# Three edits to a sparse graph transformer: attention credit at the layer border, one block weighted on VectorE, and the order of the last matmuls

## The chip, the cores and the metric

The kernel runs on one core of one Trainium2 chip. A core has five engines, each with its own instruction queue: TensorE (PE, with a separate row PEld for weight loads), VectorE (DVE), ScalarE (ACT), GpSimd (POOL) and SyncE (SP), which only issues DMAs here. Engines wait for each other through semaphores. The metric is device time in microseconds (us) of one execution.

## The reference

Two layers of the same form over 2708 tokens of 512 values, in f32, with 8 heads of 64 and a feed-forward width of 2048. A token attends to its neighbours in a graph and to itself; under 24 positions a row are open in the sparse matrix that the inputs give.

```python
def _L0_gnn_ref(h, adj, ...):
    n = h.shape[0]
    mask = adj.astype(jnp.float32) + jnp.eye(n, dtype=jnp.float32)
    q = (h @ Wq.T + bq).reshape(n, N_HEADS, D_K)
    k = (h @ Wk.T + bk).reshape(n, N_HEADS, D_K)
    v = (h @ Wv.T + bv).reshape(n, N_HEADS, D_K)
    scores = jnp.einsum('nhd,mhd->hnm', q, k) / jnp.sqrt(jnp.float32(D_K))
    scores = jnp.where(mask[None, :, :] == 0, jnp.float32(-1000000000.0), scores)
    attn = jax.nn.softmax(scores, axis=-1)
    ctx = jnp.einsum('hnm,mhd->nhd', attn, v).reshape(n, D_MODEL)
    h1 = _layer_norm(h + ctx @ Wo.T + bo, ln1_g, ln1_b)
    ff = jax.nn.relu(h1 @ W1.T + b1) @ W2.T + b2
    return _layer_norm(h1 + ff, ln2_g, ln2_b)
...
x = _L0_gnn_ref(x, adj, ...)
x = _L1_gnn_ref(x, adj, ...)
```

## The kernel before

**Tiles and slots.** A first part turns the adjacency into neighbour lists of at most 24 slots, sorts the tokens by their number of neighbours, and cuts them into 22 tiles of 128 (the last, tile 21, holds 20). Each tile has a number of slots that all its tokens fit into: tile 21 has 3, 20 has 5, 19 has 6, 18 has 7, 9 has 9, 8 has 10. Tiles go in pairs, called blocks; `blocks` is (21,20), (19,18), (8,9), (7,10), (6,11), (0,17) and so on, 11 in all. A second way over all pairs of tokens stands behind a flag and isn't executed.

**Attention** is not a matmul here. For each tile, chunk by chunk of two slots (`SLOTS`), POOL gathers the key and value rows of those neighbours into a buffer `kv` (L982, five buffers, up to three gathers ahead). DVE multiplies the keys by the query (L1019) and sums over each head (L1025), which gives scores `sc`. ACT takes exponentials (L1038) into `p`. The values are then weighted by `p`: slot 0 by one DVE product of 128x512 (L1051), slot 1 by eight ACT copies with a scale, one for each head (L1045). DVE adds the result to `acc` (L1058). At the end of a tile come the sum over slots (L1066), the largest score (L1070), the sum of `p` (L1078) and its reciprocal (L1081), and ACT divides (L1089) into `cx`. The generator `attend` issues these in a pipeline: in each step the scores of one chunk, the weighting of the chunk before, the sums of the one before that, the division of the one before that.

**Dense work** is on PE. `query` projects q into a PSUM buffer of the tag "g" (three buffers), evicts it by DVE (L1226) into a "row" buffer `qs` (three buffers, shared with `xb`), and `kept` stores it to DRAM by SP (L1236, `q_d`) when the next query is issued. `attended` turns `cx` (`flip`, tp L1128, ACT L1133) into cT, projects it with Wo (L569), and adds the residual xb (loaded at L979, added at L1254), and `norm` follows: statistics L1112 to L1116, a power on POOL L1118, and the two passes L1119 and L1122. `feed_forward` makes 16 steps f: matmuls pf (L1296), relu ft on ACT (L1304), and, three steps later (`LAG`), `second` (L1284) into one PSUM accumulator for each tile of the block. The last three steps follow tile by tile. Then come add (L1316), norm, and in the last layer the store of the output (L1319).

**How the two are woven together.** Code order is queue order on PE, ACT and SP everywhere; on POOL in the first part and layer 0; on DVE only in the first queries and at the border between the layers. Elsewhere a scheduler orders DVE. Between dense pieces the kernel calls `advance(x)`: x is added to a credit (at most 1.5), and `attend` makes steps until it is used up; a chunk of two slots costs 1, one of a single slot 0.5. No step is made while two finished `cx` wait to be used. At the border, the head of layer 1, there is one `advance(0.5)` before each of the queries (L1491 and L1494), whose zT come from DRAM by SP (L1213):

```python
while pool:
    advance(0.5)
    now.query(*pool.pop(0))
for i in range(2 * AHEAD - 10):
    advance(0.5)
    next(streamed)
through(0)
early[n] = now.attended(blocks[0], got)
```

`through(0)` makes attention steps until both tiles of the first block are divided.

Of the kernel before, what the change touches and what calls it, by code (L numbers as in the profile page):

```python
# [19 lines left out]
DM = 512  # L20
NH = 8
DK = DM // NH
# [3 lines left out]
NFC = FF // P  # L26
# [12 lines left out]
LAG = 3  # L39
# [432 lines left out]
def by_edges(ctx: ExitStack, tc: tile.TileContext, x, xT, adj, layers, out, good):  # L472
# [13 lines left out]
    NL = len(layers)  # L486
# [94 lines left out]
    def size(g):  # L581
        return min(P, N - g * P)
# [425 lines left out]
    class Tile:  # L1008


        def __init__(self, g, q):
            self.g, self.r, self.q = g, size(g), q
            self.sc = at.tile([P, LIST, NH], F32, tag="sc", name="sc", bufs=2)
            self.p = at.tile([P, LIST, NH], F32, tag="p", name="p", bufs=2)
            self.acc = None
# [16 lines left out]
        def weigh(self, kv, s0, c):  # L1032
            r, g, p = self.r, self.g, self.p
            if s0 == 0:
                self.acc = at.tile([P, SLOTS, DM], F32, tag="acc", name="acc", bufs=2)
                self.wide = c
            for s in range(s0, s0 + c):
                nc.scalar.activation(  # L1038
                    p[:r, s, :], self.sc[:r, s, :], AF.Exp, bias=minus[:r, g, s : s + 1]
                )  # L1040
            to = self.acc[:r] if s0 == 0 else kv[:r, :, DM:]
            for i in range(1, c):
                for h in range(NH):
                    hd = slice(h * DK, (h + 1) * DK)
                    nc.scalar.activation(  # L1045
                        to[:, i, hd],
                        kv[:r, i, DM + h * DK : DM + (h + 1) * DK],
                        AF.Copy,
                        scale=p[:r, s0 + i, h : h + 1],
                    )  # L1050
            nc.vector.tensor_tensor(  # L1051
                to[:, 0, :].rearrange("p (h d) -> p h d", d=DK),
                kv[:r, 0, DM:].rearrange("p (h d) -> p h d", d=DK),
                p[:r, s0, :].unsqueeze(2).to_broadcast([r, NH, DK]),
                ALU.mult,
            )
            if s0:
                nc.vector.tensor_tensor(  # L1058
                    self.acc[:r, :c, :], self.acc[:r, :c, :], kv[:r, :c, DM:], ALU.add
                )  # L1060
# [76 lines left out]
    class Layer:  # L1137
# [133 lines left out]
        def feed_forward(self, block, hs, hT):  # L1271

            w = sum(size(g) for g in block)
            accs = [ps_a.tile([P, DM], F32, tag=f"a{i}", name=f"a{i}") for i in range(len(block))]
            fts = []

            def second(f, only=None):
                c0 = 0
                for g, a in zip(block, accs):
                    r = size(g)  # L1280
                    if only not in (None, g):
                        c0 += r
                        continue
                    nc.tensor.matmul(  # L1284
                        a[:r],
                        fts[f][:, c0 : c0 + r],
                        self.w2[f // 2][:, f % 2, :],
                        start=(f == 0),
                        stop=(f == NFC - 1),
                    )  # L1290
                    c0 += r

            for f in range(NFC):
                pf = ps_f.tile([P, DM], F32, tag="f", name="pf")
                for c in range(NC):
                    nc.tensor.matmul(  # L1296
                        pf[:, :w],
                        self.w1[f // 2][:, c, f % 2 * P : f % 2 * P + P],
                        hT[:, c, :w],
                        start=(c == 0),  # L1300
                        stop=(c == NC - 1),
                    )
                ft = dn.tile([P, 2 * P], F32, tag="ft", name="ft", bufs=4)
                nc.scalar.activation(ft[:, :w], pf[:, :w], AF.Relu, bias=self.b1[:, f : f + 1])  # L1304
                fts.append(ft)
                if f >= LAG:
                    second(f - LAG)
                yield None
            for g in block:
                for f in range(NFC - LAG, NFC):  # L1310
                    second(f, g)
            zs = []
            for g, a, h in zip(block, accs, hs):
                r = size(g)
                z = h
                nc.vector.tensor_tensor(z[:r], a[:r], h[:r], ALU.add)  # L1316
                norm(z, r, self.g2, self.e2)
                if self.n == NL - 1:
                    nc.gpsimd.indirect_dma_start(  # L1319
                        out=out,  # L1320
                        out_offset=bass.IndirectOffsetOnAxis(ap=ident_i[:r, g : g + 1], axis=0),
                        in_=z[:r],
                        in_offset=None,
                        bounds_check=N - 1,
                        oob_is_err=False,
                    )
                zs.append(z)
            yield zs
# [41 lines left out]
    blocks = [(NT - 1, NT - 2), (NT - 3, NT - 4)] + [  # L1370
        (i, NT - 5 - i) for i in (*range(8, 5, -1), *range(6))
    ]
# [3 lines left out]
    def attend(n, got):  # L1376

        peak = small.tile([P, NT], F32, tag="peak", name="peak", bufs=1)
        nc.vector.memset(peak, 0.0)
        loaded = loads(n)  # L1380
        steps = []
        for g in order:
            cuts = chunks_of(g)
            steps += [(g, s0, c, i, i + 1 == len(cuts)) for i, (_, s0, c) in enumerate(cuts)]
            if g == order[1]:
                steps += [None] * 3
        steps += [None] * 3
        kv = next(loaded)
        yield 0.0
        q = asked(n, order[0])  # L1390
        done = [None] * 3
        for k, step in enumerate(steps):
            if step:
                g, s0, c, i, last = step
                if i == 0:
                    while q is None:
                        q = asked(n, g)
                        if q is None:
                            yield None
                    t, q = Tile(g, q), None  # L1400
                if k > 0:
                    kv = next(loaded)
                t.weights(kv, s0, c)
                if i > 0 and q is None and g != order[-1]:
                    q = asked(n, order[order.index(g) + 1])
                done.append((t, kv, s0, c, last))
            else:
                done.append(None)
            t3, t2, t1 = done[-4:-1]
            if t1:  # L1410
                t1[0].weigh(*t1[1:4])
            if t2 and t2[-1]:
                t2[0].sums(peak)
            if t3 and t3[-1]:
                got[t3[0].g] = t3[0].divided()
            yield c / SLOTS if step else 0.2
        nc.vector.tensor_reduce(flags[:, 4 + n : 5 + n], peak, AX.X, ALU.max)
        nc.vector.tensor_scalar(
            flags[:, 4 + n : 5 + n], flags[:, 4 + n : 5 + n], SAFE, None, ALU.is_le
        )  # L1420
# [3 lines left out]
    def advance(more):  # L1424

        nonlocal credit
        credit = min(credit + more, 1.5)
        while credit > 0 and len(got) < CXB - 1:
            cost = next(ahead, None)
            if cost is None:  # L1430
                break
            credit -= cost

    def through(k):

        while blocks[k][-1] not in got:
            next(ahead)
# [40 lines left out]
    for n in range(NL):  # L1478
        last = n == NL - 1
        nxt = None if last else Layer(n + 1, layers[n + 1])  # L1480
        if n > 0:
            streamed = now.queries(order[8 : 2 * AHEAD])
            got = {}
            ahead = attend(n, got)
            with tc.manual_schedule(engines={mybir.EngineType.DVE}):
                for _ in range(2):
                    now.query(*pool.pop(0))
                next(ahead)
                next(streamed)
                while pool:  # L1490
                    advance(0.5)  # L1491
                    now.query(*pool.pop(0))
                for i in range(2 * AHEAD - 10):
                    advance(0.5)  # L1494
                    next(streamed)
                through(0)
                early[n] = now.attended(blocks[0], got)
                next(early[n])
                for _ in blocks[0]:
                    next(early[n])  # L1500
                finish(streamed)
            now.load_w2(NFC // 2 - 1)
# [6 lines left out]
        for k, block in enumerate(blocks):  # L1509
# [4 lines left out]
            for f, zs in enumerate(now.feed_forward(block, hs, hT)):  # L1514
# [22 lines left out]
                if not last:  # L1537
# [7 lines left out]
                    if f == 1 and k in (1, 3):  # L1545
                        i, name, scale = (1, "bk", 1.0) if k == 1 else (0, "bq", DK**-0.5)
# [97 lines left out]
```

## Time and profile before

| | us |
|---|---|
| median of 3 runs | 1966.08 (1964.01 to 1967.41) |
| the profiled execution | 1964.63 |
| its span in the profile | 1962.9 |
| PE busy | 1901.0 |
| DVE busy | 1300.8 |
| ACT busy | 933.8 |
| POOL busy | 796.8 |

What one operation costs, from the page's groups (line, engine, operation, tiles, form, count, then busy us, mean ns of one, and idle time of the engine before them with what ended most of it):

```profile
L982 POOL DMA_INDIRECT kv<-kv_d,idx x420 | 546.1, 1300 | 475.9 <-DVE acc L1058 319.1
L1045 ACT ACTIVATE kv<-kv,p 128x64 f32<-128x64 f32 x1232 | 311.0, 335 | 5.0
L1058 DVE TENSOR_TENSOR acc<-acc,kv 128x1024 f32<-128x1024 f32 (+2 forms) x178 | 204.0, 1146 | 26.7 <-ACT kv L1045 25.9
L1051 DVE TENSOR_TENSOR kv<-kv,p 128x512 f32<-128x512 f32 (+1 forms) x178 | 121.6, 684 | 52.8 <-ACT p L1038 52.7
```

PE, DVE and PEclk by 40 slices of the span (49 us each; tenths, 9 is 90% or more):

```profile
PE   8999988999999999999999998999999999999997
DVE  5884587685867869659442036888688988877421
PEclk9999999999999999999999999999999999999998
```

The slices with an 8 or a 7 on PE are the first, the sixth and seventh (245 to 343 us, layer 0's first block), the 25th (1178 to 1227, the border of the layers), and the last. An instruction that is reported busy may run at a lower clock: PEclk tells of the mean over a slice, and short drops show only in windows of 10 us. The first block of layer 0 ends at about 346 us.

### The profile page before, as it was taken

What the parts mean: (1) busy time and instruction counts of PE and PEld (TensorE: products, weight loads), DVE (VectorE), ACT (ScalarE), POOL (GpSimd) and SP (SyncE); (2) the same over time, 40 slices, a digit from 0 to 9 for tenths busy, and PEclk for the clock granted to TensorE, in tenths of its full rate; (3) what the DMA queues carried; (4) which work ended last, traced back from release to release, by engine and by line L of the source; (5) the groups of instructions that cost most, each with busy time, mean ns of one, the idle gap of its engine ahead of it and who ended that gap; (6) DMA issues with size and microseconds to landing.
All of it is one profiled execution on the core that took longest, in us unless ns stands there. A gap on an engine that the chain in (4) does not pass through costs nothing. (4 is left out here: it accounts for less than half of the span.)

```text
span 1962.9 us, 20872 instructions
## 1 busy us (share of the span) xinstructions
PE 1901.0 (97%) x6162; PEld 1100.6 (56%) x6162; DVE 1300.8 (66%) x2142; ACT 933.8 (48%) x3219; POOL 796.8 (41%) x710
## 2 busy tenths in 40 slices
PE   8999988999999999999999998999999999999997
PEld 4444444565565655566556643556666566666664
DVE  5884587685867869659442036888688988877421
ACT  4660254564555655547332112756456765755410
POOL 3114635453555535425310022555347655644210
PEclk9999999999999999999999999999999999999998
DMA  9998766455655556546310646856455766554000
GB/s 327 352 311 307 258 211 235 161 166 189 202 161 199 188 186 227 161 150 204 130 43 27 230 162 215 298 174 217 153 177 198 247 214 209 186 190 154 34 11 13
DMA packets 131486, 366.92 MB, mean 187 GB/s; under 512 B 16668, under 2 KB 36988, under 8 KB 128654
## 3 DMA queue, kind: packets, MB, share of 16 engines
q0 software_dynamic: 69120, 246.35, 37.9%
q1 hardware_dynamic: 53332, 99.66, 14.9%
q10 hardware_dynamic: 8910, 19.48, 2.6%
q8 instruction: 50, 0.82, 0.2%
q14 instruction: 74, 0.61, 0.1%
HBM read 314.62 MB, written 50.83 MB: 186 GB/s over the span
## 5 line engine op out<-in xcount | busy, mean ns | idle before, releaser
L982 POOL DMA_INDIRECT kv<-kv_d,idx x420 | 546.1, 1300 | 475.9 <-DVE acc L1058 319.1
L1284 PE MATMUL a<-w,ft 128*128 128x512 f32 (+1 forms) x1408 | 669.9, 601 | 10.8 <-ACT ft L1304 9.5
L1296 PE MATMUL pf<-hT,w 128*128 128x256 f32 (+1 forms) x2816 | 636.3, 373 | 13.2 <-ACT ft L1304 8.8
L1296 PEld LDWEIGHTS pf<-hT,w 128*128 128x128 f32 x2816 | 521.1, 191 | 192.2 <-issue 107.3
L1284 PEld LDWEIGHTS a<-w,ft 128*128 128x128 f32 (+1 forms) x1408 | 256.5, 187 | 239.0 <-issue 201.4
L1304 ACT ACTIVATE ft<-pf,b 128x256 f32<-128x256 f32 (+1 forms) x352 | 158.5, 459 | 424.8 <-PE pf L1296 424.5
L1019 DVE TENSOR_TENSOR kv<-kv,q 128x1024 f32<-128x1024 f32 (+3 forms) x222 | 256.5, 1158 | 156.3 <-DMA kv<-kv_d,idx 103.7
L1045 ACT ACTIVATE kv<-kv,p 128x64 f32<-128x64 f32 x1232 | 311.0, 335 | 5.0
L1025 DVE TENSOR_REDUCE sc<-kv 128x16 f32<-128x1024 f32 (+3 forms) x222 | 255.2, 1154 | 1.4
L1058 DVE TENSOR_TENSOR acc<-acc,kv 128x1024 f32<-128x1024 f32 (+2 forms) x178 | 204.0, 1146 | 26.7 <-ACT kv L1045 25.9
L1118 POOL TENSOR_TENSOR rd<-va,mhalf 128x1 f32<-128x1 f32 (+1 forms) x88 | 85.4, 971 | 267.6 <-DVE va L1116 266.2
L1038 ACT ACTIVATE p<-sc,minus 128x8 f32<-128x8 f32 (+1 forms) x420 | 103.4, 295 | 161.1 <-DVE sc L1025 154.6
L569 PE MATMUL o<-wo,cT 128*128 128x512 f32 (+1 forms) x352 | 157.8, 601 | 3.7 <-DVE qs L1226 3.3
L1051 DVE TENSOR_TENSOR kv<-kv,p 128x512 f32<-128x512 f32 (+1 forms) x178 | 121.6, 684 | 52.8 <-ACT p L1038 52.7
L569 PEld LDWEIGHTS o<-wo,cT 128*128 128x128 f32 (+1 forms) x352 | 65.5, 187 | 92.2 <-issue 80.9
L1089 ACT ACTIVATE cx<-acc,su 128x64 f32<-128x64 f32 (+1 forms) x352 | 88.4, 333 | 42.6 <-DVE su L1081 33.9
L1316 DVE TENSOR_TENSOR h<-a,h 128x512 f32<-128x512 f32 (+1 forms) x44 | 29.7, 677 | 106.8 <-PE a L1284 106.7
L1122 DVE SCALAR_TENSOR_TENSOR h<-h,rd,ln_b 128x512 f32<-128x512 f32 (+1 forms) x88 | 65.9, 749 | 50.9 <-POOL rd L1118 50.9
L663 ACT ACTIVATE code<-aj 128x2708 bf16<-128x2708 int32 (+1 forms) x22 | 73.2, 3329 | 49.1 <-POOL aj L659 45.4
L1355 POOL DMA_INDIRECT kv_d<-kvs,ident_i x22 | 23.7, 1077 | 179.0 <-ACT kvs L1349 110.9
L666 DVE MAX8 tops<-code 128x8 f32<-128x247 f32 (+2 forms) x242 | 83.1, 400 | 19.3 <-ACT code L663 19.3
L1045 ACT ACTIVATE acc<-kv,p 128x64 f32<-128x64 f32 (+1 forms) x352 | 88.8, 334 | 1.4
(133 smaller groups left out, 1514.2 us busy)
## 6 DMA issues: line engine op xcount, KB each, us to landing
aj<-in_adj SPq DMA_DIRECT2D x21, 1354.0 KB, 8.0
kv_d<-kvs ACTq DMA_DIRECT2D x21, 512.0 KB, 5.6
w<-in_W SPq DMA_DIRECT2D x20, 512.0 KB, 4.8
xg<-in_xT SPq DMA_DIRECT2D x19, 512.0 KB, 8.8
kv<-kv_d,idx POOLq DMA_INDIRECT x420, 5.6
w<-in_W ACTq DMA_DIRECT2D x12, 512.0 KB, 8.9
q_d<-qs SPq DMA_DIRECT2D x22, 256.0 KB, 4.2
zT_d<-zT SPq DMA_DIRECT2D x22, 256.0 KB, 5.3
```

Of the source, the lines that this page charges most:

```text
L569: nc.tensor.matmul(o[:r], xs(c), wm[:, c, :], start=(c == 0), stop=(c == NC - 1))
L982: nc.gpsimd.indirect_dma_start(out=to, out_offset=None, in_=table[:, :], in_offset=bass.IndirectOffsetOnAxis(ap=s, axis=0), bounds_check=N ...
L1019: nc.vector.tensor_tensor(kv[:r, :c, :DM], kv[:r, :c, :DM], self.q[:r].unsqueeze(1).to_broadcast([r, c, DM]), ALU.mult,)
L1025: nc.vector.tensor_reduce(self.sc[:r, s0 : s0 + c, :], kv[:r, :c, :DM].rearrange("p s (h d) -> p s h d", d=DK), AX.X, ALU.add,)
L1038: nc.scalar.activation(p[:r, s, :], self.sc[:r, s, :], AF.Exp, bias=minus[:r, g, s : s + 1])
L1045: nc.scalar.activation(to[:, i, hd], kv[:r, i, DM + h * DK : DM + (h + 1) * DK], AF.Copy, scale=p[:r, s0 + i, h : h + 1],)
L1051: nc.vector.tensor_tensor(to[:, 0, :].rearrange("p (h d) -> p h d", d=DK), kv[:r, 0, DM:].rearrange("p (h d) -> p h d", d=DK), p[:r, s0, : ...
L1058: nc.vector.tensor_tensor(self.acc[:r, :c, :], self.acc[:r, :c, :], kv[:r, :c, DM:], ALU.add)
L1089: nc.scalar.activation(cx[:r, hd], self.acc[:r, 0, hd], AF.Copy, scale=self.su[:r, h : h + 1])
L1284: nc.tensor.matmul(a[:r], fts[f][:, c0 : c0 + r], self.w2[f // 2][:, f % 2, :], start=(f == 0), stop=(f == NFC - 1),)
L1296: nc.tensor.matmul(pf[:, :w], self.w1[f // 2][:, c, f % 2 * P : f % 2 * P + P], hT[:, c, :w], start=(c == 0), stop=(c == NC - 1),)
L1304: nc.scalar.activation(ft[:, :w], pf[:, :w], AF.Relu, bias=self.b1[:, f : f + 1])
```

## The change

It has three parts. At the border both `advance(0.5)` become `advance(0.4)`. A tile gets a flag `alone`, true for the tiles of the second block (19 and 18) in layer 0: DVE then weighs all the slots of a chunk in one product (128x1024 instead of 128x512), and ACT makes no copies for it. And in the last block of the last layer, in the last step f = 15, `second(12)` is issued for the first tile alone; the second tile's f = 12 is issued ahead of its 13, 14 and 15, after all of the first tile's.

```diff
@@ class Tile
-        def __init__(self, g, q):
+        def __init__(self, g, q, alone=False):
             self.g, self.r, self.q = g, size(g), q
+            self.alone = alone
@@ Tile.weigh
             to = self.acc[:r] if s0 == 0 else kv[:r, :, DM:]
-            for i in range(1, c):
+            e = c if self.alone else 1
+            for i in range(e, c):
                 for h in range(NH):
...
             nc.vector.tensor_tensor(
-                to[:, 0, :].rearrange("p (h d) -> p h d", d=DK),
-                kv[:r, 0, DM:].rearrange("p (h d) -> p h d", d=DK),
-                p[:r, s0, :].unsqueeze(2).to_broadcast([r, NH, DK]),
+                to[:, :e, :].rearrange("p s (h d) -> p s h d", d=DK),
+                kv[:r, :e, DM:].rearrange("p s (h d) -> p s h d", d=DK),
+                p[:r, s0 : s0 + e, :].unsqueeze(3).to_broadcast([r, e, NH, DK]),
                 ALU.mult,
             )
@@ feed_forward
                 if f >= LAG:
-                    second(f - LAG)
+                    very_last = self.n == NL - 1 and block == blocks[-1] and f == NFC - 1
+                    second(f - LAG, block[0] if very_last else None)
                 yield None
             for g in block:
-                for f in range(NFC - LAG, NFC):
+                for f in range(NFC - LAG - (very_last and g != block[0]), NFC):
                     second(f, g)
@@ attend
-                    t, q = Tile(g, q), None
+                    t, q = Tile(g, q, n == 0 and g in blocks[1]), None
@@ the border
                 while pool:
-                    advance(0.5)
+                    advance(0.4)
                     now.query(*pool.pop(0))
                 for i in range(2 * AHEAD - 10):
-                    advance(0.5)
+                    advance(0.4)
                     next(streamed)
```

## Prediction

> **What bounds the kernel now.** I read the page first: span, busy shares, PE's slices.
>
> ```profile
> span 1962.9 us, 20872 instructions
> PE 1901.0 (97%) x6162; PEld 1100.6 (56%) x6162; DVE 1300.8 (66%) x2142; ACT 933.8 (48%) x3219; POOL 796.8 (41%) x710
> ```
>
> PE is busy in 97% of the span, so 1962.9 − 1901.0 = 61.9 us is all that can be won without taking matmuls away, and the change takes none away. Then the waits of PE, to see who ends that idle time:
>
> ```profile
> PE a L1284 <- ACT ft L1304: 9.5, 9, 2.8
> PE pf L1296 <- ACT ft L1304: 8.8, 4, 3.5
> PE tp L1128 <- DVE h L1122: 4.3, 2, 3.9
> PE o L569 <- DVE qs L1226: 3.3, 1, 3.3
> PE q L569 <- DVE qs L1226: 2.9, 2, 1.7
> ```
>
> (us in total, times, longest.) They sit where the three edits sit. So I read PE's timeline in those places; brackets hold the idle time before an entry and its releaser. Layer 0, first block's feed-forward:
>
> ```profile
> 277.66 2.34 PE L1296 MATMUL pf<-hT,w 128*128 128x148 f32 x8 [2.81 <-ACT ft L1304]
> 279.93 3.90 PE L1284 MATMUL a<-w,ft 128*20 128x512 f32 x4
> 293.35 1.79 PE L1296 MATMUL pf<-hT,w 128*128 128x148 f32 x8 [3.45 <-ACT ft L1304]
> 299.62 1.27 PE L1296 MATMUL pf<-hT,w 128*128 128x148 f32 x8 [1.38 <-ACT ft L1304]
> 333.12 1.11 PE L1128 MATMUL tp<-ident,h 128*128 128x128 f32 x4 [3.86 <-DVE h L1122]
> 334.17 7.58 PE L1284 MATMUL a<-w,ft 128*20 128x512 f32 x12
> ```
>
> A long stall costs twice: eight pf matmuls take 1.17 us elsewhere in this block, but 2.34 and 1.79 behind the stalls of 2.81 and 3.45. The layer border, all engines:
>
> ```profile
> 1201.47 1.22 DVE L1226 SCALAR_TENSOR_TENSOR qs<-q,bq 128x512 f32<-128x512 f32 x2
> 1202.13 0.32 SPq L1236 DMA_DIRECT2D q_d<-qs  x1
> 1202.15 3.70 PE L569 MATMUL q<-wq,zT 128*128 128x512 f32 x8 [1.21 <-DVE qs L1226]
> 1209.23 0.69 DVE L1226 SCALAR_TENSOR_TENSOR qs<-q,bq 128x512 f32<-128x512 f32 x1 [5.83 <-DMA q_d<-qs]
> 1210.07 6.30 PE L569 MATMUL o<-wo,cT 128*20 128x512 f32 x8 [3.27 <-DVE qs L1226]
> 1210.39 1.66 SPq L979 DMA_DIRECT2D xb<-xb_d  x2
> 1216.41 0.68 DVE L1254 TENSOR_TENSOR h<-o,xb 20x512 f32<-20x512 f32 x1 [6.49 <-PE o L569]
> 1227.33 1.01 PE L1128 MATMUL tp<-ident,h 20*128 20x20 f32 x8
> 1228.88 4.31 PE L1296 MATMUL pf<-hT,w 128*128 128x148 f32 x32 [0.54 <-ACT hT L1133]
> ```
>
> Read this as one chain: a query evicted at 1201.47 is stored at 1202.13; its buffer ("row", three of them) is free at 1209.23, when the last query can be evicted; only then has o (1210.07) a PSUM buffer. The tail:
>
> ```profile
> 1942.51 7.03 PE L1284 MATMUL a<-w,ft 128*128 128x512 f32 x16
> 1947.01 0.69 DVE L1316 TENSOR_TENSOR h<-a,h 128x512 f32<-128x512 f32 x1 [47.81 <-PE a L1284]
> 1950.62 0.68 DVE L1316 TENSOR_TENSOR h<-a,h 128x512 f32<-128x512 f32 x1
> ```
>
> [...] stalls of 2.81, 3.27, 3.45 and 3.86 are followed by slow matmuls (o: 6.30 for 3.70), those of 1.21, 1.38 and 1.74 hardly. [...] That is how attention reaches PE here: relu (ft) stands in ACT's queue behind exponentials that wait for DVE's scores. [...] The trace has means of 684 (L1051) and 1146 to 1158 (L1058, L1019, which mix in a few narrower ones); I use the trace.
>
> **Part two, block (19,18) by DVE alone.** Tile 19 has three chunks of two slots, tile 18 three of two and one of one: six products grow from 128x512 to 128x1024. Their pitch on DVE is 0.60 now (295.08 to 295.68), that of a 128x1024 operation 1.14 (292.21, 293.34, 294.48): 6 × 0.54 = +3.2 us on DVE. Off ACT go 6 × 8 = 48 copies, 2.02 us a set, pitch about 1.93: −11.6 us. No cover is assured: DVE is 10.0 of 10 busy in 270–280. The instruction orders show the same sets on PE, POOL and SP, and on DVE a few exchanges in this stretch: the second weighting of tile 18 goes before the score reduction of the next tile, 8. Replayed step by step:
> - The first product lies before L1122 at 263.57: feed-forward starts 0.54 later (265.49 to 266.0).
> - Two more make tile 18's first scores 0.5 to 1 late; but the eight copies ahead of the relu at 277 are gone: stall of 2.81 to about 2.1. The division of tile 19 is 0.75 late, so the next relu is 0.8 late: a new stall of about 2.6.
> - Tile 8's gather is issued 0.6 late and lands at 288.65 for 288.10; its score now also waits for one weighting (1.13): its exponentials at 292.15 for 290.49. The relu behind them: PE goes on at 295.0 for 293.35. The following stall (299.62) moves by about +1.1 to +1.7. Up to here PE loses some 1.5.
> - In exchange that weighting ends earlier, so its accumulation ends at 293.25 for 294.56 and frees a kv buffer 1.3 sooner. Through POOL's gathers tile 9's first chunk lands at 315.7 for 316.92, and DVE reaches L1122 (332.31) 1.2 earlier.
> - PE at 333.12 waits for just that, and its 3.86 us of idle swallow the 1.5 lost before: tp at 331.9.
>
> Net −1.2. What follows (the slow a x12, 7.58 for about 5.3) could give 2.4 more if the stall of now some 1.5 spares the clock; I count none of it, since PE waits for a kvs eviction of the same DVE chain at 376. Bounds: −3 (clock spared and kept), +2.5 (buffer comes no earlier, the extra DVE time enters most of the way).
>
> **Part one, 0.4 at the border.** DVE is ordered by hand there, so smaller credit moves instructions: one eviction qs goes ahead of nine DVE instructions of a chunk and a finished tile. PE's, POOL's, SP's and ACT's orders stay, so no DMA issue is moved past another.
> - That qs runs right behind the qs of 1195.34 and the accumulation's end, at 1197.1 for 1201.47, as q is ready. Two 0.67 us evictions no longer follow each other at 1201.47; the q of 1202.15 starts when the 16 before it end (1193.84 + 7.10): 1200.95. −1.2.
> - Its store is issued at 1197.8 for 1202.13. Now it took 1209.23 − 1202.13 = 7.1 to free the buffer; the same from 1197.8 is 1204.9, when the last query (1200.95 + 3.70 = 1204.65) is just ready. So the last qs runs at 1204.9, not 1209.23.
> - The attention instructions go behind it; the division (1201.63) is 0.65 later, its ACT work at 1204.9 for 1206.24 anyway. o starts at 1205.7 for 1210.07, with an idle time too short to slow the clock: 3.44 for 6.30; end 1209.15 for 1216.37.
> - What is late next: h needs xb too. The two xb loads need "row" buffers of qs whose stores go out at 1202.9 and 1203.9, 6 to 7 us each: loads at 1209 to 1210 (now 1210.39), landing by an estimate of 4 us from the median of such loads and stores (4.2 to 5.3 on the page) at 1213 to 1214. So h at 1213.6, not 1209.3: −2.8. The last o and the 16 q matmuls (1216.83, 1220.37) don't wait for h: q ends near 1220.3, tp follows at 1221.7 behind both norms and the next qs, pf at 1222.75 for 1228.88.
>
> −6.1. Bounds: −3 if the stores land late, so that h binds at 1216; −7 if xb is early and the 16 q bind alone.
>
> **Part three, the tail.** One f32 second matmul of 512 is two records of 0.43, so 0.86. Tile 0's sum ends 0.86 earlier (its add at 1946.15 for 1947.01), tile 1's where it was (1942.51 + 7.03 = 1949.54). Tile 1's add stood at 1950.62 behind tile 0's L1122 of 1949.95, not behind PE; so it comes at 1949.76, still after 1949.54. −0.86; bounds −0.5 and −0.9.
>
> **Sum.** −1.2 − 6.1 − 0.9 = −8.2. The profiled execution took 1964.63 (span 1962.9 and 1.7 around it): 1956.4. The median shown is 1.45 above it: 1957.9, rounded 1958.
>
> **Rivals.**
> - A, the border's gain is capped: the stall moves from the qs store to the stores ahead of xb, which land late while DMA is 0.88 busy (1200–1210). For: 7.1 us for a store is far above the median 4.2. Against: in 1210–1220 DMA share is 0.22. Border −2, others −1: 1963. 17%.
> - B, the work of PE before the border is early, but attention's gathers set layer 1's pace, so the gain comes back as waits of 1 to 3 us (there are some at 1430, 1520, 1620), or block 0 loses what the border gains: 1964 to 1968, centre 1966. For: those waits exist. Against: PE is hardly idle for 200 us behind the border, long enough for attention to lead. 13%.
> - C, slower: DVE carries block 0's chain. The +3.2 enters whole, [...] With three more slow stretches at 2.9: 3.2 + 8.7 = +11.9, less 7.0 of the others: +4.9, 1971. It decides once block 0 loses over 7.0 and is slower beyond measuring at 10.9. For: DVE at 10.0 of 10, the new 2.6 stall. Against: 3.86 us of PE idle at 333 that absorb it, and 11.6 us off ACT. 10%.
> - D, block 0 spares its clock and keeps it, border at its best: −3 − 7 − 0.9 = −10.9: 1955. 12%.
>
> **Numbers.** The forecast 48%, A 17, B 13, C 10, D 12. About 0.2% (3.9 us) is what a measurement of this kernel can tell from no change: faster means under 1962.2, slower over 1970. Faster: 48 + 12 + about 8 of A + 2 of B = 70%; slower: 9 of C + 1 of B = 10%; same 20%. Range 1954 to 1965: it holds the forecast's own bounds, D's and A's, and leaves out C and most of B.
>
> **What would show it.** Right: the last qs of the border near 1205, o at full clock behind under 1.5 us idle, pf some 6 us earlier relative to the span; a last L1316 0.9 earlier; in block 0 a tp wait for h under 2 us. Wrong: slow matmuls (PEclk under 0.9) in more slices of 270–300 than now; h at the border waiting for xb to 1216; later waits on ft or q_d in layer 1 that give the 6 us back.

## The result, and the profile after

| | before | after |
|---|---|---|
| median of 13 runs each | 1966.74 us | 1962.70 us |
| lowest and highest | 1963.51, 1970.56 | 1956.50, 1966.42 |
| the profiled execution | 1964.63 | 1965.94 |

The ratio is 0.9974, with a 95% interval of 0.9964 to 0.9985: the change saves 5.1 us by the ratio (3.0 to 7.1), 4.0 by the medians. The forecast was 1958, thus 8.2 us less; direction and range held, and the gain by the ratio is about six tenths of that, by the medians half. In a later set of runs, on another occasion, the same kernel had a ratio of 0.9988 (0.9977 to 0.9998).

The profiled execution of the changed kernel is one of its slowest, 1.3 us longer than that of before. So spans can't be compared; stretches can. PE's matmuls stand in the same order in both kernels up to the last 16, so matmul number k of one trace can be laid beside number k of the other. How much later each begins than in the profile before (us):

```
matmul   at (before)   what begins there                  after is later by
    0         4.9      first key projection                     -0.2
  488       212.2      first part, near its end                 +1.4
  627       264.1      just ahead of block 0's feed-forward     +1.7
  728       299.6      block 0, behind its ft stalls            +4.6
  852       339.9      block 0, behind its tp stall             +2.4
 3595      1185.6      queries of the border                    +6.5
 3680      1228.9      layer 1, first pf                        +0.7
 6145      1942.9      second of the last 16 matmuls            +2.4
```

Read it downwards: what matters is the change from line to line. Of the 6.5 us that after is late at 1185, 1.7 come from the first part, which the change doesn't touch, 0.8 from block 0, and about 4 from the feed-forward blocks behind it. Between 1185 and 1230 it wins 5.8. First the page and PE's waits of after:

```profile
span 1964.1 us, 20821 instructions
PE 1901.4 (97%) x6162; PEld 1101.5 (56%) x6162; DVE 1304.3 (66%) x2142; ACT 922.6 (47%) x3171; POOL 796.8 (41%) x710
```

```profile
PE pf L1298 <- ACT ft L1306: 10.6, 3, 7.5
PE a L1286 <- ACT ft L1306: 10.0, 9, 2.8
PE tp L1130 <- DVE h L1124: 4.4, 3, 2.5
PE q L569 <- DVE qs L1228: 2.3, 1, 2.3
```

(Line numbers are one to three higher than before.) DVE is busy 3.5 us more, ACT 11.2 less: 3.2 and 11.6 were forecast. The wait of o for qs, 3.3 us before, is gone; but one wait of pf for ft now lasts 7.5. The timeline of after at the border, PE's entries and those of DVE and SP that the chain runs through:

```profile
1196.74 15.82 PE L569 MATMUL q<-wq,zT 128*128 128x512 f32 x32 [2.29 <-DVE qs L1228]
1204.13 0.67 DVE L1228 SCALAR_TENSOR_TENSOR qs<-q,bq 128x512 f32<-128x512 f32 x1
1204.83 0.32 SPq L1238 DMA_DIRECT2D q_d<-qs  x1
...
1212.50 1.01 PE L1130 MATMUL tp<-ident,cx 20*128 20x20 f32 x8
1212.60 0.69 DVE L1228 SCALAR_TENSOR_TENSOR qs<-q,bq 128x512 f32<-128x512 f32 x1 [2.10 <-PE q L569]
1213.44 3.60 PE L569 MATMUL o<-wo,cT 128*20 128x512 f32 x8
1214.92 1.66 SPq L979 DMA_DIRECT2D xb<-xb_d  x2
1217.19 0.68 DVE L1256 TENSOR_TENSOR h<-o,xb 20x512 f32<-20x512 f32 x1 [3.90 <-DMA xb<-xb_d]
...
1221.04 7.03 PE L569 MATMUL q<-wq,zT 128*128 128x512 f32 x16
1228.00 1.01 PE L1130 MATMUL tp<-ident,h 20*128 20x20 f32 x8
```

The qs of 1204.13 is the one that moved. The last qs (1212.60) now waits for its own matmuls, not for a store; o follows tp at once, at full clock (the eight in 3.60 us, granted clock 1.00 from 1213.44 to 1217.1). As forecast, h waits for xb now, 3.9 us. But that wait costs nothing: the 16 q matmuls end at 1228.0, and tp begins there without a wait. Block 0 of layer 0, PE's timeline of after:

```profile
278.94 1.81 PE L1298 MATMUL pf<-hT,w 128*128 128x148 f32 x8 [1.88 <-ACT ft L1306]
284.77 1.27 PE L1298 MATMUL pf<-hT,w 128*128 128x148 f32 x8 [0.94 <-ACT cx L1091]
298.62 2.34 PE L1298 MATMUL pf<-hT,w 128*128 128x148 f32 x8 [7.52 <-ACT ft L1306]
336.38 0.66 PE L1130 MATMUL tp<-ident,h 128*128 128x128 f32 x4 [2.52 <-DVE h L1124]
```

Beside the places of before: 2.81 became 1.88; a stall of 0.94 is new; 3.45 became 7.52; the 1.38 behind it is gone; 3.86 became 2.52. And the tail:

```profile
1944.91 7.03 PE L1286 MATMUL a<-w,ft 128*128 128x512 f32 x16
1948.54 0.69 DVE L1319 TENSOR_TENSOR h<-a,h 128x512 f32<-128x512 f32 x1 [46.94 <-PE a L1286]
1952.16 0.69 DVE L1319 TENSOR_TENSOR h<-a,h 128x512 f32<-128x512 f32 x1
```

From the start of the last 16 matmuls to the second add: 7.25 us, 8.11 before. That is the 0.86 of the forecast.

### The profile page after: what moved, and what is told of

Read it like the earlier page. It is cut to its first block, busy times and chain, and to the rows that moved or that the text cites. A ratio compares the mean times of both kernels' runs of the same rounds, so it can differ in the third digit from the quotient of the medians.

```text
span 1964.1 us, 20821 instructions
## 1 busy us (share of the span) xinstructions
PE 1901.4 (97%) x6162; PEld 1101.5 (56%) x6162; DVE 1304.3 (66%) x2142; ACT 922.6 (47%) x3171; POOL 796.8 (41%) x710
## 5 line engine op out<-in xcount | busy, mean ns | idle before, releaser
L1047 ACT ACTIVATE kv<-kv,p 128x64 f32<-128x64 f32 x1200 | 302.9, 335 | 4.9
L1053 DVE TENSOR_TENSOR kv<-kv,p 128x512 f32<-128x512 f32 (+2 forms) x178 | 123.6, 695 | 52.6 <-ACT p L1039 52.6
L569 PE MATMUL k<-wk,xg 128*128 128x512 f32 (+1 forms) x176 | 81.9, 609 | 5.7 <-DMA wk<-in_Wk 4.7
```

The source lines that it names most:

```text
L569: nc.tensor.matmul(o[:r], xs(c), wm[:, c, :], start=(c == 0), stop=(c == NC - 1))
L1047: nc.scalar.activation(to[:, i, hd], kv[:r, i, DM + h * DK : DM + (h + 1) * DK], AF.Copy, scale=p[:r, s0 + i, h : h + 1],)
L1053: nc.vector.tensor_tensor(to[:, :e, :].rearrange("p s (h d) -> p s h d", d=DK), kv[:r, :e, DM:].rearrange("p s (h d) -> p s h d", d=DK), p ...
```

## The experiments

Each kernel ran in rounds with the kernel before on the same chip; ratios are to that. Beside the time, each profile was laid over that of before as above, and three stretches were taken out of it. They are given together behind the experiments.

**The three parts, each alone.** First the border's 0.4 without the rest:

```diff
-                    t, q = Tile(g, q, n == 0 and g in blocks[1]), None
+                    t, q = Tile(g, q), None
-                    very_last = self.n == NL - 1 and block == blocks[-1] and f == NFC - 1
+                    very_last = False
```

> The border's 0.4 alone; block (19,18) is weighted as before and the last matmuls stand in the old order. Theory 1 (the prediction): 6.1 us faster than before (range 3 to 7), since the eviction no longer sits behind nine attention instructions. Theory 2 (the two profiles: PE is 6.6 us late ahead of the border and 0.7 behind it): 5 to 6 us faster, so the border gave about what was forecast and the loss lies elsewhere. Theory 3 (the border's gain is drawn from PE having been late when it came, and nothing else): 0 to 2 us faster.

Measured: 0.9980 (0.9970 to 0.9990), which is 3.9 us less (2.0 to 5.9); the border stretch is 5.6 us shorter than in the profile before. Theory 3 is excluded by the profile and only just by the times. Theory 2's 5 to 6 us fit the profile; by the times the middle lies below both figures (6.1; 5 to 6), but the interval reaches into theory 2's and into theory 1's range of 3 to 7, so the two aren't told apart.

Next the second part alone: both credits at 0.5 and the last matmuls in the old order.

```diff
-                    advance(0.4)
+                    advance(0.5)
...
-                    very_last = self.n == NL - 1 and block == blocks[-1] and f == NFC - 1
+                    very_last = False
```

> Only block (19,18) by DVE alone; border and tail as before. Theory 1: 1.2 us faster (3 faster to 2.5 slower). Theory 2: 2 to 4 us slower, with PE's wait for ft near 298 us grown to 5 us or more, and later feed-forward blocks of layer 0 starting 2 to 4 us later than before. Theory 3: no difference over 1 us, the late PE of the profile being the first part's spread from run to run.

Measured: 0.9998 (0.9989 to 1.0006), so between 2.2 less and 1.2 more. Theory 2's 2 to 4 us of loss are excluded. Theory 1's gain of 1.2 lies inside the interval, and so does none (theory 3). In this profile the third stall was 4.81, not 7.5.

The third part alone:

```diff
-                    advance(0.4)
+                    advance(0.5)
...
-                    t, q = Tile(g, q, n == 0 and g in blocks[1]), None
+                    t, q = Tile(g, q), None
```

> Only the order of the last matmuls. All theories: 0.9 us faster, which is at the limit of what the times tell; in the profile the first tile's L1316 add begins 3.4 us after PE's last 16 matmuls began and not 4.5, and the second add directly follows the first tile's L1122.

Measured: 0.9995 (0.9982 to 1.0007): a gain of 0.9 can't be told from none by time. In its profile the last 16 begin at 1953.10, the adds at 1956.74 and 1960.35: 3.64 and 7.25 behind them (4.50 and 8.11 before), close to the 3.4 expected for the first.

Border and tail, without the second part:

```diff
-                    t, q = Tile(g, q, n == 0 and g in blocks[1]), None
+                    t, q = Tile(g, q), None
```

> The change without its second part (ACT makes slot 1's copies of block (19,18) again). Theory 1: 7.0 us faster than before, 1.2 slower than the changed kernel. Theory 2: 6 to 7 us faster than before, 2 to 4 us faster than the changed kernel, and so the best of all so far. Theory 3: 1 to 3 us faster than before.

Measured: 0.9974 (0.9963 to 0.9984), 5.1 us less (3.2 to 7.3). The same ratio as the whole change in its first set of runs, so the second part adds nothing to it that could be seen.

**Is it the store's wait?** The border's mechanism can be had without touching the order: the query that waited gets another buffer.

```diff
-            qs = dn.tile([P, DM], F32, tag="row", name="qs", bufs=3)
+            far = self.n > 0 and g == order[2 * AHEAD - 1]; qs = dn.tile([P, DM], F32, tag="h" if far else "row", name="qs", bufs=4 if far else 3)
```

> The kernel before with one buffer moved: the last query projected at the border is evicted into a buffer of the tag h and not into the third row buffer, so that it need not wait until an earlier query is stored. All five engines' orders stay as before, credit 0.5 too. Theory A (the 7 us of that store bound the border, the 0.4 only started it earlier): DVE's wait of 5.8 us for q_d<-qs is gone, o begins within 1.5 us behind tp, and the stretch from the border's queries to pf is 4 to 6 us shorter, nearly as with 0.4; time 3 to 5 us less than before. Theory B (what counts is that evictions no longer stand behind attention's instructions on DVE): the stretch is shorter by 2 us at most.

Measured: 0.9998 (0.9987 to 1.0008). This edit missed its aim: it moved the 16th query, and the one that waits is the 14th. DVE's timeline shows it, the wait is still there, and the moved query is evicted long after (1226.58):

```profile
1211.08 0.69 DVE L1226 SCALAR_TENSOR_TENSOR qs<-q,bq 128x512 f32<-128x512 f32 x1 [4.90 <-DMA q_d<-qs]
1223.31 0.69 DVE L1226 SCALAR_TENSOR_TENSOR qs<-q,bq 128x512 f32<-128x512 f32 x1
```

So the run says nothing of the two theories. It serves as one more profile of the old border, and a useful one: here o took 3.59 us behind a stall of 2.35, not 6.30 as in the profile before. Its companion, with 0.4 and the tail's order, missed in the same way and serves as a second run of border and tail:

> The border's 0.4 and the tail's order, with the last border query in a buffer of the tag h as in the run beside it. Theory A: with 0.4 the stores no longer bind PE, so only the xb loads come some us earlier, which PE covers with 16 q matmuls: no more than 0.5 us less at the border, the same time as border and tail alone. Theory B: the same. A gain of over 2 us would show that the store still bound something behind 0.4.

Measured: 0.9966 (0.9953 to 0.9979), 6.7 us less.

The same with the right query (the index is now `2 * AHEAD - 3`), credit 0.5, tail and second part as before:

```diff
-            far = self.n > 0 and g == order[2 * AHEAD - 1]; qs = ...
+            far = self.n > 0 and g == order[2 * AHEAD - 3]; qs = ...
```

> The kernel before with the right query moved: the query evicted last ahead of o (the 14th in tile order) goes into a buffer of the tag h and not into a row buffer; the run before had moved the 16th, which is evicted behind o. All orders and credit 0.5 stay. Theory A (the wait for the store bound PE): DVE's wait for q_d<-qs ahead of o is gone, o begins within 1 us behind tp, the border stretch is 3 to 5 us shorter than in the kernel before. Theory B (the place of the evictions among attention's instructions counts): shorter by 2 us at most, though that wait is gone.

Measured: 0.9985 (0.9978 to 0.9992), 2.9 us less (1.6 to 4.3); the border stretch is 5.5 us shorter than in the profile before. The timeline, DVE and PE:

```profile
1209.83 0.69 DVE L1226 SCALAR_TENSOR_TENSOR qs<-q,bq 128x512 f32<-128x512 f32 x1 [2.49 <-PE q L569]
1210.67 3.60 PE L569 MATMUL o<-wo,cT 128*20 128x512 f32 x8
1215.18 0.68 DVE L1254 TENSOR_TENSOR h<-o,xb 20x512 f32<-20x512 f32 x1 [4.65 <-DMA xb<-xb_d]
```

No eviction was moved, only the buffer, and the stretch is as short as with 0.4. DVE's instructions stand in the same order at the border as before. Theory A holds, theory B falls: the 7 us of the store bound the border, and what 0.4 does is to start that store earlier.

The same buffer with 0.4 and the tail's order:

> Border 0.4 and tail, with the same query in a buffer of the tag h. Theory A: the store no longer binds PE once 0.4 has started it earlier, so the border stretch differs by less than 0.7 us from border and tail alone. Theory B: the same. If xb behind the stores still mattered, h would come 2 to 3 us earlier and PE with it; expected is that only h comes earlier, since 16 q matmuls stand ahead of tp.

Measured: 0.9976 (0.9969 to 0.9983); the border stretch is 5.2 shorter, 1.2 us longer than that of border and tail alone (6.4 shorter), where under 0.7 was expected. The difference arises ahead of tp, where the queries waited 2.9 us and then ran slowly (32 of their matmuls took 15.85 us; 16 took 7.03 behind o); o follows tp at once in both. The xb loads were issued at 1206.25, no longer behind the stores, and h waited for o again, not for xb; PE gained nothing by it. So the new wait for xb costs nothing here.

**Less credit still:**

```diff
-                    advance(0.4)
+                    advance(0.3)
```

(at both places of the border, with the tail's order, without the second part)

> Border and tail with 0.3 for 0.4: three more evictions go ahead of attention's instructions, attention is later. Theory A: queries are no longer late at all, but the division of the first block's tiles comes 2 to 4 us later and tp waits for cx: 0 to 3 us slower than with 0.4. Theory B: another 1 to 3 us faster, since each eviction that stands ahead of attention frees PE.

Measured: 1.0021 (1.0011 to 1.0031), 4.1 us slower than before; the stretch is 4.2 longer than in the profile before. PE's timeline shows where: with more evictions ahead of attention's instructions a query is late first (3.87), and then cx is late (3.78).

```profile
1197.74 13.45 PE L569 MATMUL q<-wq,zT 128*128 128x512 f32 x24 [3.87 <-DVE qs L1228]
1212.25 0.39 PE L1130 MATMUL tp<-ident,cx 20*128 20x20 f32 x4 [1.05 <-DVE qs L1228]
1216.42 1.91 PE L1130 MATMUL tp<-ident,cx 128*128 128x128 f32 x4 [3.78 <-ACT cx L1091]
```

The late cx is what theory A said; that queries would no longer be late was not so. Against border and tail it loses 9 to 11 us, three times theory A's upper end or more. Theory B falls.

**What DVE's extra time costs.** The larger dose, all tiles of layer 0 by DVE alone, border and tail as before:

```diff
-                    t, q = Tile(g, q), None
+                    t, q = Tile(g, q, n == 0), None
```

> A larger dose of the second part: all tiles of layer 0 are weighed by DVE alone (border and tail as before). There are 198 sets of copies in two layers, so some 99 here: 99 x 0.54 = +53 us on DVE and 99 x 1.93 = -191 us on ACT, spread over 900 us. Theory 1 (DVE's extra time lies beside PE, which is why six products cost nothing): within 3 us of before. Theory C (DVE carries the chain through the gathers where PE waits): 5 us slower or more, by longer waits for ft and h in layer 0.

Measured: 1.0080 (1.0061 to 1.0100), 15.7 us slower. Theory 1 falls. PE's waits in this profile (totals over the span):

```profile
PE pf L1298 <- ACT ft L1306: 13.4, 5, 7.4
PE tp L1130 <- DVE h L1124: 12.5, 6, 5.3
```

In the profile before these were 8.8 and 4.3. DVE works 50 us more (1351.1 for 1300.8) and ACT 196 less (737.4 for 933.8); about 0.3 us of each of the 50 reach the end. By an estimate at that rate six products, 3.2 us, would cost 1.

**The second part once more.** The changed kernel again, and a version that weighs only tile 18 on DVE, in one set of runs with the one above.

> The changed kernel again, for a second profile of it and times beside those of border and tail. Theory 1 (the second part gains 1.2): 6.5 to 8 us faster than before. Theory 2 (the second part gives and takes about the same): 4.5 to 6 us faster; in block 0 the first ft stall near 1.9, the stall behind tile 8's exponentials at 5 us or more (3.1 to 5.2 without the second part), the tp wait near 2.5.

Measured: 0.9988 (0.9977 to 0.9998), 2.4 us less (0.4 to 4.5): below both theories' figures. The profile is as theory 2 said: 1.89, 7.17, and 2.28 at tp.

```diff
-                    t, q = Tile(g, q, n == 0 and g in blocks[1]), None
+                    t, q = Tile(g, q, n == 0 and g == blocks[1][1]), None
```

> Border and tail as changed, but of block (19,18) only tile 18 is weighed by DVE alone: three larger products instead of six. Theory 1 (each larger product that lies ahead of L1122 or of scores costs its 0.54): feed-forward of block 0 starts without the 0.5 us delay, the first ft stall is about 1.9 again, and the stretch over block 0 is 0.5 to 1.5 us shorter than in the changed kernel. Theory 2 (the gather's landing decides block 0): no difference that the stretch, which spreads by about 1 us, could show.

Measured: 0.9975 (0.9967 to 0.9984), 4.9 us less. Feed-forward began without the 0.5 delay and the first stall was 0.76, better than expected; the later ones were 2.60, 6.00 and 2.21. The stretch over block 0 was 1.3 to 1.9 us shorter than in two profiles of the changed kernel, and 1.0 longer than in the profile of the second part alone. So theory 1 isn't told from theory 2.

**The stretches, all profiles.** Block 0 is from matmul 500 to 852, the border from 3590 to 3680; each is the time against the profile before. The third column is the stall behind tile 8's exponentials, the fourth the wait of tp for h.

```
                            block 0   ft stall   tp stall   border
without the second part, credit 0.5
  before                      0.0       3.45       3.86       0.0
  tail alone                 -1.2       4.10       4.13      +0.7
  16th query moved           -1.5       4.16       4.03      -3.1
  14th query moved           -0.2       4.30       3.64      -5.5
without the second part, credit 0.4 (the last: 0.3)
  border alone               +1.1       4.97       4.34      -5.6
  border and tail            -1.3       4.17       3.86      -6.4
  the same, 16th moved       -0.6       5.24       3.61      -6.2
  the same, 14th moved       +0.6       4.54       4.23      -5.2
  border 0.3 and tail        -0.1       3.09       4.25      +4.2
with the second part
  second part alone, 0.5     -2.1       4.81       2.33      -1.5
  the change                 +0.8       7.52       2.52      -5.8
  the change again           +0.2       7.17       2.28      -5.4
  tile 18 only, 0.4          -1.1       6.00       2.21      -5.8
  all of layer 0, 0.5        +8.2       7.44       4.15      -3.3
```

None of the versions is shown to beat the changed kernel: border and tail without the second part had 0.9974, 0.9966 and 0.9976 in three sets of runs, the change 0.9974 and 0.9988, and the intervals overlap.

## Why the prediction was right in direction and too large in size

**The border, its mechanism: right in the main link.** The chain from the early eviction over the store to o held at each link, and moving one buffer instead of one instruction gave the same. The new wait for xb came too. Two smaller steps did not, and they offset each other by luck. The step "the q of 1202.15 starts when the 16 before it end" (−1.2) failed: the queries ahead of tp waited 2.29 us once and then ran at a lowered clock (32 of their matmuls took 15.82 us, with 0.89 granted on the mean; the 16 of 1221.04 took 7.03, with 1.00), so the tp of cx came 0.2 later than before, counted from matmul 3590. In the seven profiles with 0.4 it begins 22.0 to 23.1 us behind that matmul, in the five of the old order 22.3 to 23.0. And what the forecast took as late next (tp behind both norms and the next qs, 1.4 us behind the q matmuls) was not late: tp begins where the 16 q matmuls end.

**The border, its size: the term "3.44 for 6.30" was mis-sized.** It was worked out against the one profile of before, in which all eight o matmuls were slow behind the 3.27 us stall (granted clock 0.50 from 1210 to 1215, where PEclk's slice of 49 us still has a 9). In the old order these took 6.30, 6.47, 5.04, 3.59 and 3.59 us in five profiles (the last is the version with all of layer 0), and the border's stretch went with them: 0, +0.7, −1.5, −3.1 and −3.3, a mean of −1.4. Seven profiles with 0.4 lie between −5.2 and −6.4, with a mean of −5.8. The gain over a mean execution is therefore about 4.4, not 6.1. On its own profile the forecast came near (5.8 against 6.1), in part by the luck just named, and that profile was a bad draw in this place.

**Part two: the step that failed is "Tile 8's gather is issued 0.6 late and lands at 288.65".** POOL's timeline in block 0 (the start, the time of the issue itself, the wait ahead of it), first of before:

```profile
272.53 1.97 POOL L982 DMA_INDIRECT kv<-kv_d,idx  x1 [0.30 <-DVE kv L1019]
...
276.09 1.88 POOL L982 DMA_INDIRECT q<-q_d,ident_i  x1 [0.30 <-issue]
278.27 1.07 POOL L982 DMA_INDIRECT kv<-kv_d,idx  x1 [0.30 <-ACT p L1038]
```

The same stretch of POOL's timeline, of after:

```profile
274.91 2.87 POOL L982 DMA_INDIRECT kv<-kv_d,idx  x1 [0.74 <-DVE acc L1060]
...
279.37 2.41 POOL L982 DMA_INDIRECT q<-q_d,ident_i  x1 [0.30 <-issue]
282.08 1.07 POOL L982 DMA_INDIRECT kv<-kv_d,idx  x1 [0.30 <-issue]
```

The last line of each is the first of two gathers for tile 8's second chunk; the other follows 1.38 later in both, and DVE waits for the later of the two before it goes on to the scores of the first chunk. Feed-forward begins at 265.49 and 267.70 there, so the gather comes 12.8 and 14.4 us behind it: 1.6 later, and 0.54 more as feed-forward itself begins later. That is 2.1 where 0.6 was forecast. The replay had looked at when POOL is released, and had left the two issues ahead as long as they were: they took 2.87 and 2.41 us where before had 1.97 and 1.88. The other profile of the change has 2.86 and 2.41, and the same 14.4; the nine profiles without the second part have 12.8 each. DVE went on at 292.17 where before had 288.10: less the 1.67 of the first part that is 2.4 later, where 0.55 was forecast.

What stretches an issue can be read from DVE's timeline. That of after in this stretch:

```profile
274.56 2.35 DVE L1020 TENSOR_TENSOR kv<-kv,q 128x1024 f32<-128x1024 f32 x2
279.08 1.21 DVE L1053 TENSOR_TENSOR acc<-kv,p 128x1024 f32<-128x1024 f32 x1
280.21 0.68 DVE L1068 TENSOR_TENSOR acc<-acc 128x512 f32<-128x512 f32 x1
```

The issue of 274.91 began in the two key products and ended 0.87 us behind the second (276.91); that of 279.37 began in tile 18's enlarged product and ended 0.89 behind the sum that follows it (280.89). In all 14 profiles together POOL issued 6132 gathers of kv and q. All 2764 that began while DVE ran an instruction with two tensor inputs and took over 1.2 us ended 0.80 to 0.95 us behind the end of such an instruction; of the 2319 that began while DVE was idle or ran anything else, 33 took over 1.2 us, and their median is 1.00. So in these traces an issue that falls on such an instruction waits it out, sometimes the next one too. No run was made to test this, but it holds through every trace. The enlarged product thus has a price on POOL which the prediction put at nothing: it stretched the issue of q from 1.88 to 2.41, and in the version with tile 18 alone to 2.40. The other 0.9 came since POOL's issue fell on the first of the two key products, and not on the second as before.

In the profile of the second part alone, which is the same code in this place, POOL's timeline has these two issues shorter:

```profile
277.04 1.72 POOL L982 DMA_INDIRECT kv<-kv_d,idx  x1 [0.74 <-DVE acc L1060]
280.36 1.01 POOL L982 DMA_INDIRECT q<-q_d,ident_i  x1 [0.30 <-issue]
```

The first began 0.36 into the pair of key products, as in after, but ended 0.87 behind the first of them; the second then fell on a reduction. The gather came at 12.9, with the 0.54 just the 0.6 of the forecast; its stall was 4.81. So the forecast's value does occur, and so does a worse one. What lets an issue through between two products in one execution and not in another is not shown. The next step, tile 8's scores standing behind one more weighting, was right: DVE's order is that in each of these profiles. In the two profiles of the change PE went on behind the stall 3.6 and 3.2 us later than before, less what the first part cost, where 1.65 was forecast.

**Part two, the other steps: right in part.** Feed-forward began 0.54 later; the first stall was 1.88 for about 2.1; the new stall was 0.9, where 2.6 was forecast, since the copies ahead of the division were gone too. Behind that, "DVE reaches L1122 (332.31) 1.2 earlier" came only in the profile of the second part alone (1.3 earlier); in the two of the change it was 1.6 and 1.0 later, and PE waited there 2.5 and 2.3 us, not under 2. The idle time ahead of tp still shrank from 3.9, and with it a part of the loss: matmuls 728 to 852 gained 2.2 to 2.4 against before in the three profiles with all six products, about 0.8 of it by a higher clock (tp 0.66 for 1.11 and the 12 second matmuls 7.22 for 7.58; over both, 0.78 granted in the change's first profile and 0.69 in that of before), and 0.2 on the mean in the others. So 0.54 and a mean of 1.4 were lost (2.4, −0.3, 2.1 over matmuls 628 to 728), and 2.3 won back: about 0.4 in all, where 1.2 was forecast. The block's stretch as a whole has a mean of −0.4 with the second part (three profiles) and of −0.4 without it (nine, the 0.3 among them); the change's own two have +0.8 and +0.2.

**Part three: right**, 0.86 in each profile with it.

**The sum.** 4.4 + 0.9 + 0 = 5.3 on the profiles' means, where 8.2 was forecast; with block 0 from the change's own two profiles alone (0.9 slower than the nine without the second part) it is 4.4. By the times the change has 5.1 (3.0 to 7.1) in one set and 2.4 (0.4 to 4.5) in the other. What stays open is whether the second part costs 1 to 2 us further on: the rate of the large dose would give 1; from matmul 852 to 3590 the change is later than the profile before by 4.1 and 1.2, the second part alone by 3.1 and tile 18 only by 7.3, the nine without it by 0 to 5.1 with a mean of 2.0; in the last set the change lies 0.12% behind the two versions with none or half of it, within the error, and the profiles are too few.

**The rivals.** A named the right new wait (xb), but it bound nothing. B, gains given back in layer 1, isn't seen: from matmul 3680 to 6150 the seven profiles with 0.4 are later than before by a mean of 1.1 (−1.1 to +2.1), the six with 0.5 by 0.6 (−0.1 to +1.8), half a microsecond apart by the means and less than the profiles spread. C, DVE carrying block 0's chain, names what the large dose showed: stalls grew to 7.4 there, and block 0 lost 8.2. (Its 2.9 for a slow stretch is an estimate from the profile before: the pf and second matmuls behind the stalls of 2.81 and 3.45 took 3.0 and 1.7 us more than elsewhere in block 0.) With six products block 0 lost 0.8 and 0.2 in the change's two profiles, since the idle time ahead of tp takes up most of their loss. D's spared clock behind tp came only for a moment (tp 0.66 for 1.11, in all three profiles with six products, though in two of the others too), and was part of the 2.3; the 12 second matmuls behind it still took 7.22 us for 7.58, not the 5.3 that D needs, and in no profile under 6.4.

The forecast's terms for a slowed clock rest on the stalls of one profile. Behind the same stall of 2.81 in block 0, eight pf took 2.34, 1.77, 1.85 or 1.27 us in different profiles whose code is the same in this place, and the four second matmuls behind them from 2.09, as elsewhere, to 3.90. What makes the difference is not shown. So what a long stall costs differs from execution to execution, and has to be entered as a mean.

## What to carry to other kernels

A term that is read from one profile and consists of a slowed clock behind a stall should be entered at its mean over several executions (for o about half of the excess that the one profile had). When a replay runs through an engine that issues gathers, the time of an issue is no constant (1.0 to 2.9 us in block 0 of the two profiles above): look which of VectorE's instructions it falls on, and give whatever queues behind two of them a range, not a value. Before an order is tuned around a wait for a buffer, move the one user to another buffer: here that showed the mechanism with every instruction order left alone.

## What the runs showed of the hardware that was not expected

A store of 256 KB at the border kept its source buffer for about 7 us from issue (1202.13 to 1209.23), while the median landing of such stores is 4.2 on the page. Stalls as short as 1.9 us were followed by slowed matmuls in block 0 (eight pf 1.81 and 2.33 us behind 1.88 and 1.89; in a third profile 1.27 behind 1.89, but 3.72 for 2.09 in the four second matmuls next), while at the border eight q took 3.70 behind 2.00, 2.26 and 2.38 in three profiles, as eight o matmuls do there behind 0.46. The first part, up to matmul 500, is the same code in all versions and differed by up to 7.9 us between profiles (−1.8 to +6.1 against that of before). A gather's issue on GpSimd took 1.00 us by the median, or, where it fell on a VectorE instruction with two tensor inputs, mostly until 0.87 us behind that instruction's end; with all of layer 0 on VectorE the first 210 gathers of kv took 1.33 us each on the mean, 1.24 to 1.28 in the other 13 profiles.
